# Decoder block on one core: the first token tile of x loaded as two partition halves, issued from SP and from ACT

## The chip, the cores and the metric

The kernel runs on one core of one Trainium2 chip. A core has five engines with an instruction queue each: PE (TensorE, matrix multiplication, with its weight loads shown apart as PEld), DVE (VectorE), ACT (ScalarE), POOL (GpSimd) and SP (SyncE, which here only issues DMA transfers). They run side by side and meet at semaphores; each takes its own instructions strictly in order. DMA transfers between device memory (DRAM) and the core's on-chip memory (SBUF) are issued by an engine's queue and carried out by 16 DMA engines.

The metric is the device time of one execution in microseconds, the median of several runs.

## What is computed

A decoder block on x of shape (8, 112, 512): self-attention, cross-attention to a context, and a gated feed-forward layer, each on a layer norm of x and added to x. Cut to its skeleton, the reference is:

```python
x = x + attn(_layernorm(x), Wq, bq, Wk, bk, Wv, bv, Wo, bo)   # 16 heads, rope, causal, softmax
x = x + xattn(_layernorm(x), ctx, Wq, Wkv_expand, Wout)       # keys and values from ctx, causal
x = x + ffn(_layernorm(x), w_gating, w_linear)                # fp8: gelu(x@w0) * (x@w1) @ w_linear

def _layernorm(x, axis=-1, eps=1e-05):
    m = jnp.mean(x, axis=axis, keepdims=True)
    v = jnp.var(x, axis=axis, keepdims=True)
    return (x - m) / jnp.sqrt(v + eps)
```

Only the very first step, the layer norm of the first 128 tokens, is touched here.

## The kernel before

The 8 x 112 = 896 tokens are treated as 7 tiles of 128 tokens, one token per partition, 512 float32 values (2 KB) each. All of x stays in SBUF as `x_sb` (line 243). Lines 256 and 257 load it, one transfer of 128 partitions and 256 KB per tile, through `load` (line 251), which issues on `nc.sync`, SP's queue. Every other load and every copy inside SBUF that goes by DMA is issued by SP as well; ACT issues none. Three large feed-forward weights are issued by POOL later on.

All work is first written down as a numbered list of operations (`op`, line 57). The text `ORDER` (line 102) then gives the order in which they are emitted, and so each engine's queue. The beginning reads `1 23-24 37 26 40 25 43 85-87 94 22 88 0 89 95-98 90 2-19 91 ...`. Number 1 is a fill of a zero tile by DVE. Numbers 23 to 29 are the loads of x tiles 0 to 6, numbers 37, 40 and 43 the first three quarters of Wv, so SP issues: x tile 0, x tile 1, Wv 0, x tile 3, Wv 1, x tile 2, Wv 2, then Wv 3, the mask, x tiles 6 and 5, Wq 0, and so on. Numbers 2 to 19 are 18 matrix multiplications on the zero tile (line 239, `warm`), which stand at the head of PE's queue.

The path of the first tile, by line:

- line 252, SP: the load; in the trace of the program before, its issue is the first of SP.
- line 300, DVE: `bn_stats` on the tile, then 301 and 302 (mean, variance plus epsilon).
- line 303, POOL: the power -1/2; line 306, DVE: the bias.
- line 307, ACT: the normalised tile `xna`. The load of ACT's function table is placed ahead of it, and the wait for the x tile stands on that table load.
- line 345, PE: four 128 x 128 transposes by `ident`; then the same for tile 1, whose `xna` ACT makes right after the cast of Wv 0 (line 277).
- lines 320 and 321, ACT and DVE: the transposed tile is split into a rounded part `fmh` and a rest `fml`.
- line 359, PE: three matrix multiplications for each product (high by high, low by high, high by low), first for the values with Wv, then the queries and keys with Wq and Wk.

Each weight quarter lands in a staging tile `wst` (line 276), ACT makes the rounded part (277), POOL or DVE the rest (279).

Two mechanisms tie transfers together. Staging tiles come from a set of four (`"ws": 4` in line 98), so a later weight's load waits until an earlier one has been split. And the built program gives every transfer one of eight completion semaphores in turn, whatever queue issues it; an issue first waits until the transfer eight places before it has landed. In the program before, SP's ninth issue (the mask) is the first with such a wait: it waits for x tile 0, the tenth for x tile 1, the twelfth (Wq 0) for x tile 3.

Of the kernel before, what the change touches and what calls it, by code (L numbers as in the profile page):

```python
# [50 lines left out]
class Plan:  # L51
# [5 lines left out]
    def op(self, eng, fn, r=(), w=()):  # L57
        o = Op()
        o.eng, o.fn, o.dma, o.bufs = eng, fn, eng == "sp", []
        for b in dict.fromkeys(k[0] if isinstance(k, tuple) else k for k in (*r, *w)):  # L60
            if isinstance(b, Buf) and b.tags:
                o.bufs.append(b)
                b.left += 1
        self.ops.append(o)
        return o
# [121 lines left out]
def kernel(  # L187
# [5 lines left out]
    nc = tc.nc  # L193
# [9 lines left out]
    op = plan.op  # L203
# [21 lines left out]
    def fixed(t):  # L225
        b = Buf((), None)
        b.ap = t
        return b
# [14 lines left out]
    x_sb = fixed(act.tile([128, NT, D], F32, name="x_sb"))  # L243
# [7 lines left out]
    def load(dst, src, w, r=()):  # L251
        op("sp", lambda: nc.sync.dma_start(out=dst(), in_=src), r=r, w=w)  # L252

    xt = x.rearrange("b s d -> (b s) d").rearrange("(n p) d -> p n d", p=128)
    ot = out.rearrange("b s d -> (b s) d").rearrange("(n p) d -> p n d", p=128)
    for i in range(NT):
        load(lambda i=i: x_sb()[:, i, :], xt[:, i, :], [(x_sb, i)])

    def constant(name, src, shape):
        t = fixed(const.tile(shape, F32, name=name))  # L260
# [396 lines left out]
```

## Time and profile before

| what | value |
|---|---|
| median of 3 runs | 280.43 us (280.15 to 281.84) |
| the profiled execution | 280.48 us, of which the span from first to last instruction is 278.7 us |
| granted TensorE clock | 1.000 |
| PE busy | 273.8 us (98% of the span) |
| DVE, ACT, POOL busy | 214.6, 198.0, 114.4 us |
| transfers | 21.66 MB, 18740 packets, mean 78 GB/s |
| x transfers | 7, each 256 KB, 2.7 us (the first) to 5.8 us from issue to landing |

How to read it: times in the trace count from the first instruction. In the timeline a line gives start, length, engine, line of the kernel, operation, destination and sources, how many were merged, and in brackets the idle time before with what ended it ("the releaser"). "SPq" is SP's queue of transfers; its lengths are those of the issuing, not of the transfer. Time from issue to landing is given in the list of transfers. The chain of waits is followed back from the last instruction; a piece on it has what preceded it as its cause.

### The profile page before, as it was taken

To read this page: it belongs to the slowest core of one execution; us is meant where nothing else is said; L and a number is where in the kernel's file an instruction comes from. 1 tells how busy PE (TensorE), PEld (TensorE's weight loads), DVE (VectorE), ACT (ScalarE), POOL (GpSimd) and SP (SyncE) were. 2 spreads that over 40 slices of the span, in tenths; PEclk is the share of its full clock that TensorE was granted. 3 is DMA by queue.
4 is the path that set the end of the run, shared out by engine and by line. 5 is a ranking of instruction groups with operands and counts; after the bars stand their busy time and mean duration, and the time that the engine had idled before them with its cause. 6 is when DMAs were issued, how large, how long until landed. Compare 5 with 4: busy or idle time off the path is not lost.

```text
span 278.7 us, 7204 instructions
## 1 busy us (share of the span) xinstructions
PE 273.8 (98%) x2472; PEld 213.7 (77%) x2472; DVE 214.6 (77%) x910; ACT 198.0 (71%) x713; POOL 114.4 (41%) x126
## 2 busy tenths in 40 slices
PE   8999999999999999999999999999999999999995
PEld 3688988888887888789888877788888786555454
DVE  3673887899997989996587899989958786573843
ACT  3754141777999999970799999998997756574601
POOL 2787428427784476826532553625410110000100
PEclk9999999999999999999999999999999999999999
DMA  7955753032240413297499500020010100000005
GB/s 220 345 198 167 227 188 111 35 111 83 85 135 3 129 40 115 19 103 66 35 110 108 56 2 2 2 40 5 0 39 2 40 19 2 0 1 2 38 38 188
DMA packets 18740, 21.66 MB, mean 78 GB/s; under 512 B 7056, under 2 KB 11536, under 8 KB 18704
## 3 DMA queue, kind: packets, MB, share of 16 engines
q1 hardware_dynamic: 15584, 18.07, 20.9%
q0 software_dynamic: 3120, 3.15, 12.5%
q8 instruction: 19, 0.31, 0.5%
q14 instruction: 17, 0.14, 0.2%
HBM read 22.39 MB, written 1.84 MB: 87 GB/s over the span
## 4 chain that ended last, share of the span: by engine, by line
PE 88%; DMA 7%; ACT 2%; SPq 1%; issue 0%; POOL 0%; DVE 0%; ACTq 0%; POOLq 0%
PE psm L359 40%; PE psfg L568 18%; PE pspt L439 9%; PE psfo L593 9%; PE pss L416 6%; PE psav L449 5%; DMA wst<-in_Wk_dram 3%; DMA wst<-in_Wq_dram 2%; PE psm L345 2%; DMA x_sb<-in_x_dram 2%; ACT P L428 1%; SPq L252 1%; POOL wqwl L279 0%; ACT xna L307 0%; ACT fmh L320 0%
## 5 line engine op out<-in xcount | busy, mean ns | idle before, releaser
L428 ACT ACTIVATE P<-P,at 112x112 f32<-112x112 f32 x256 | 96.6, 383 | 10.7 <-DVE at L425 10.5
L432 POOL TENSOR_TENSOR P<-P,at 112x448 f32<-112x448 f32 x51 | 48.1, 947 | 53.8 <-DVE at L431 42.7
L425 DVE CUSTOM_DVE_ANT_0 P<-pss,mask 112x112 f32<-112x112 f32 x256 | 56.0, 266 | 2.6 <-PE pss L416 2.3
L428 ACT ACTIVATION_READ_ACCUMULATOR P<-P,at 112x1 f32 x256 | 49.4, 193 | 0.0
L439 PE MATMUL pspt<-ident,P 112*112 112x112 f32 x256 | 36.1, 263 | 0.0
L439 PEld LDWEIGHTS pspt<-ident,P 112*112 112x112 f32 x256 | 26.9, 133 | 9.5 <-issue 2.7
L316 ACT CAST gf<-psfg 128x384 bf16<-128x384 f32 (+1 forms) x45 | 22.9, 530 | 13.7 <-PE psfg L568 13.6
L568 PE MATMUL psfg<-x,wgwl 128*128 128x256 fp8e4 (+1 forms) x192 | 28.7, 291 | 0.0
L568 PE MATMUL psfg<-x,wgwh 128*128 128x256 fp8e4 (+1 forms) x192 | 28.0, 291 | 0.0
L568 PEld LDWEIGHTS <-wgwh 128*128 128x128 fp8e4 x192 | 18.4, 98 | 7.2 <-issue 1.0
L568 PEld LDWEIGHTS <-wgwl 128*128 128x128 fp8e4 x192 | 18.4, 98 | 7.0 <-issue 0.8
L578 DVE TENSOR_TENSOR gf<-gf 128x512 bf16<-128x512 bf16 (+1 forms) x32 | 12.6, 402 | 12.9 <-ACT gf L576 6.9
L316 ACT COPY pts<-pspt 112x448 f32<-112x448 f32 x36 | 18.9, 526 | 4.5 <-PE pspt L439 4.3
L425 DVE DVE_READ_ACCUMULATOR2_ANT at<- 112x1 f32 x256 | 21.3, 83 | 0.0
L576 ACT ACTIVATE gf<-gf 128x512 bf16<-128x512 bf16 (+1 forms) x32 | 17.6, 579 | 5.1 <-DVE gf L316 5.0
L316 DVE COPY pts<-pspt 112x448 f32<-112x448 f32 x28 | 17.3, 618 | 2.7 <-PE pspt L439 2.2
L416 PE MATMUL pss<-k,q 32*112 32x112 f32 x512 | 16.9, 268 | 0.0
L416 PEld LDWEIGHTS pss<-k,q 32*112 32x112 f32 x512 | 14.0, 172 | 3.1 <-issue 2.3
L599 POOL TENSOR_TENSOR x_sb<-x_sb,ob 128x512 f32<-128x512 f32 x1 | 1.2, 1230 | 35.9 <-ACT ob L316 35.9
L593 PE MATMUL psfo<-wlin,a 128*128 128x512 fp8e4 x64 | 15.8, 379 | 0.0
L449 PE MATMUL psav<-pts,v_sb 112*32 112x112 f32 x512 | 15.6, 262 | 0.0
L431 DVE RECIPROCAL at<-at 112x4 f32<-112x4 f32 x64 | 10.8, 172 | 4.9 <-ACT P L428 4.2
(139 smaller groups left out, 612.0 us busy)
## 6 DMA issues: line engine op xcount, KB each, us to landing
qt<-qs SPq DMA_DIRECT2D x32, 112.0 KB, 2.0
x_sb<-in_x_dram SPq DMA_DIRECT2D x7, 256.0 KB, 4.4
out_dram<-x_sb SPq DMA_DIRECT2D x6, 256.0 KB, 2.1
wst<-in_Wv_dram SPq DMA_DIRECT2D x4, 256.0 KB, 5.4
wst<-in_Wq_dram SPq DMA_DIRECT2D x4, 256.0 KB, 5.4
wst<-in_Wk_dram SPq DMA_DIRECT2D x4, 256.0 KB, 4.7
wst<-in_Wo_dram SPq DMA_DIRECT2D x4, 256.0 KB, 3.6
wst<-in_WoutT_dram SPq DMA_DIRECT2D x4, 256.0 KB, 3.2
```

The lines of the kernel that those rows point to most:

```text
L316: lambda e: A.copy(dst(), src()) if e == "act" else V.tensor_copy(dst(), src()), r=r, w=w)
L359: T.matmul(out=out(), lhsT=l(a), rhs=r(b), start=q == 0, stop=q == 3 * tot - 1)
L416: T.matmul(out=banks[r]()[:S, j * S : (j + 1) * S], lhsT=qk[0]()[rs, c, t0 : t0 + S], rhs=qk[1]()[rs, c, t0 : t0 + S], start=True, stop=True)
L425: op("dve", lambda ps=ps, r=r, j=j, Pv=Pv, sm=sm: V.tensor_tensor_reduce(Pv()[:, r, :], ps()[:S, j * S : (j + 1) * S], mask(), -SCALE, BIG ...
L428: op("act", lambda r=r, Pv=Pv, sm=sm: A.activation(Pv()[:, r, :], Pv()[:, r, :], AF.Exp, bias=sm()[:S, r : r + 1], scale=-1.0, accum_out=s ...
L432: op(("pool", "dve"), lambda e, sm=sm, Pv=Pv: LO[e].tensor_tensor(Pv(), Pv(), sm()[:S, 8:12].unsqueeze(2).broadcast_to([S, 4, S]), ALU.mul ...
L439: T.transpose(pt()[:S, r * S : (r + 1) * S], Pv()[:, r, :], ident()[:S, :S])
L449: T.matmul(out=av()[r * 32 : (r + 1) * 32, c * S : (c + 1) * S], lhsT=v_sb()[:, b, h * 32 : (h + 1) * 32], rhs=pts()[:S, r * S : (r + 1) * ...
L568: T.matmul(out=ps()[:, j * n : (j + 1) * n], lhsT=wg()[i][:, c, (m + j) * 128 : (m + j + 1) * 128], rhs=x8()[:, c, t0:t1], start=(c == 0), ...
L576: op("act", lambda gb=gb: A.activation(gb()[:, :w], gb()[:, :w], AF.Gelu_apprx_tanh), w=[(gf, 0)])
L578: op("dve", lambda gb=gb, fb=fb: V.tensor_tensor(fb()[:, :w], gb()[:, :w], fb()[:, :w], ALU.mult), r=[(gf, 0)], w=[(gf, 1)])
L593: T.matmul(out=ps()[:, :wd], lhsT=a8()[:, m, s], rhs=wl()[0][:, m, hs], start=(m == 0), stop=(m == NH - 1))
```

## The change

The loads of tiles 1 to 6 stay as they are. The load of tile 0, at the same place in the order, becomes two transfers of 64 partitions and 128 KB each: partitions 0 to 63 issued on SP's queue, partitions 64 to 127 on ACT's queue, where the issue is now ACT's first instruction.

```diff
+    def first_tile():
+
+        for queue, h in ((nc.sync, slice(0, 64)), (nc.scalar, slice(64, 128))):
+            queue.dma_start(out=x_sb()[h, 0, :], in_=xt[h, 0, :])
+
     for i in range(NT):
-        load(lambda i=i: x_sb()[:, i, :], xt[:, i, :], [(x_sb, i)])
+        if i:
+            load(lambda i=i: x_sb()[:, i, :], xt[:, i, :], [(x_sb, i)])
+        else:
+            op("sp", first_tile, w=[(x_sb, 0)])
```

In the built program nothing else moves: PE, DVE and POOL have the same instructions in the same order, ACT has one more (430 against 429), SP as many transfers as before. The waits change in these places: ACT's table load waits for both halves; SP's eighth issue (Wv 3), which had no wait, waits for the first half; the ninth (the mask) for the second half. From the tenth on each issue waits for the same transfer as before. Lines behind the change are 8 higher.

## The prediction

> **What bounds the kernel now.** I read the page's busy shares first: PE is busy for 273.8 of 278.7 us, so it has 4.9 us of idle time in all, and whatever the change brings has to come out of PE's waits near the start. Next I read the chain of waits, in order of time, for the first 45 us:
>
> ```profile
> 0.74 0.41 SPq L252
> ...
> 2.14 4.44 DMA x_sb<-in_x_dram
> ...
> 6.60 5.55 DMA wst<-in_Wq_dram
> ...
> 12.54 5.75 DMA wst<-in_Wk_dram
> ...
> 19.62 3.98 DMA wst<-in_Wk_dram
> ...
> 24.15 0.82 ACT xna L307
> ...
> 25.02 0.66 PE psm L345 x4
> ```
>
> The chain starts at SP's issues and runs through transfers to 23.60 us, where PE takes over. The x transfer on it is not tile 0. It is the one issued at 2.14 us, the fourth of SP's queue, which is tile 3; its landing lets SP issue Wq 0, and so on. Tile 0 is on the chain only by the 0.41 us that SP spends on issuing it. Then the timeline of the first 16 us, for the path of tile 0 itself:
>
> ```profile
> 0.74 0.88 SPq L252 DMA_DIRECT2D x_sb<-in_x_dram  x2
> 1.19 6.54 PE L239 MATMUL pswarm<-zero 128*128 128x512 bf16 x18 [1.19 <-DVE zero L236]
> 3.45 0.69 DVE L300 BATCH_NORM_STATS2 lna<-x_sb 128x6 f32<-128x512 f32 x1 [2.31 <-DMA x_sb<-in_x_dram]
> 3.50 1.28 ACT L307 ACT_TABLE_LOAD   x1 [3.50 <-DMA x_sb<-in_x_dram]
> ...
> 5.54 0.81 ACT L307 ACTIVATE xna<-x_sb,lna 128x512 f32<-128x512 f32 x1 [0.76 <-DVE lna L306]
> ...
> 6.26 0.60 ACT L277 CAST wvwh<-wst 128x512 fp32r<-128x512 f32 x1
> ...
> 6.77 0.81 ACT L307 ACTIVATE xna<-x_sb,lna 128x512 f32<-128x512 f32 x1
> ...
> 7.36 1.01 PEld L345 LDWEIGHTS psm<-ident,xna 128*128 128x128 f32 x8
> 7.57 1.04 PE L345 MATMUL psm<-ident,xna 128*128 128x128 f32 x8
> ```
>
> The reader is to see two things. Tile 0 has landed by 3.45 us, and its normalised form is ready at 5.54 + 0.81 = 6.35 us. But PE does not take it before 7.36 us, because 18 warm-up matmuls, started by DVE's zero fill and not by x, stand ahead of it in PE's queue until then. So the tile waits for PE for 1.01 us, and PE does not wait for the tile. Last, the busy time by stretches of 1 us, for the DMA share (last but one column) and GB/s (last):
>
> ```profile
> 1.00:2.00 1.00, 0.81 (x2) 0.28 (x3) 0.13 (x1) 0.00 (x0) 0.00 (x0) 1.00 0.22 53
> 2.00:3.00 1.00, 1.00 (x4) 0.43 (x3) 0.00 (x0) 0.00 (x0) 0.00 (x0) 1.00 0.95 277
> 3.00:4.00 1.00, 1.00 (x4) 0.33 (x3) 0.55 (x1) 0.50 (x1) 0.00 (x0) 1.00 1.01 260
> ```
>
> From 2 us on the 16 DMA engines are full (shares of 0.95 and 1.01, and about 1.0 up to 16 us). The bytes of the start are the same before and after, so the train of transfers can only move if its beginning moves.
>
> **The change part by part.** *SP's first issue becomes one of 64 partitions.* Would it be shorter? SP's issues last 0.33 to 0.43 us in the first 13 us. The 0.33 us occurs for 2 KB (bk_t) and for 256 KB (the x tile at 8.44 us) alike, and the mask of 112 partitions took 0.43. So the size of the transfer does not set it. Ends: 0.08 us less (0.41 to 0.33), 0.02 more (0.43); I take 0, since the neighbours at 1.21 and 1.66 us show 0.42 and 0.43. SP's later issues then keep their places, and the chain above its start.
>
> *ACT issues the other half as its first instruction.* No row shows an issue on ACT. Bounds by SP's issues: 0.33 to 0.63 us (the copy to v_sb at 17.77 us). Queued behind it are the table load and everything ACT does; but ACT is idle until 3.50 us, so an issue that starts by about 0.9 us (DVE's first instruction is at 0.86) ends before 1.6 us. It costs 0. If that cover were gone, the 0.76 us in which ACT waits for DVE's L306 after its table load (4.78 to 5.54) would be next.
>
> *The landing of tile 0,* now the later of two halves. Early end: the nearest transfers of half the size, the 112 KB copies qt<-qs, land 2.0 us after issue, where tile 0 took 2.7; that is 0.7 us less, so 2.74 us in place of 3.44. Late end: ACT's half takes as long as Wv 0, the fourth in line at the start, 4.2 us from issue to landing; so 4.94 us, 1.5 us later. I take 2.7 us, no difference: the row is tile 0 itself, which has the DMA engines to itself until tile 1 is issued at 1.21 us, and two halves bring the same 256 KB to the same 16 engines.
>
> What is each worth? Early: DVE's L300, ACT's table load and `xna` of tile 0 move up by as much, and PE still comes at 7.36 us. Tile 1, the second four transposes, gains nothing either, since PE does the two tiles one after the other. Worth 0 for any gain in the landing. Late by L: the table load, `xna` 0, the cast of Wv 0 and `xna` 1 are one queue on ACT, almost without gaps from 5.54 to 7.58 us, so all move by L. The first four transposes stand 1.01 us off. The second four start about half-way through the weight loads' 1.01 us, at 7.36 + 0.5 = 7.86, and `xna` 1 is ready at 7.58: a slack of about 0.3 us. So the price on PE is L - 0.3 us: nothing up to L = 0.3, and 1.2 us at L = 1.5. From 9.45 to 25 us PE runs almost without gaps, so I let nothing of it be won back. Sum for the landing: 0, bounds 0 and +1.2 us.
>
> *Trainium skill, against the row.* The row of the 112 KB copies says that half the size lands 0.7 us sooner. The Trainium skill, page "DMA: Bandwidth & Descriptors", section "Rules for kernel authors", speaks against this very change: of two transfers to disjoint halves of the partitions it says "Don't bother", since both halves are spread over all 16 DMA engines, from two issuing engines as interleaved rings, and it advises one transfer of 128 partitions. By the rule tile 0 would land as before, at 3.44 us, and by the row at 2.74; the sum is the same by both, since PE does not wait for tile 0.
>
> *New waits.* SP's eighth issue, Wv 3, now waits for SP's half, and the ninth, the mask, for ACT's half. Before, SP came to Wv 3 at 4.03 us and to the mask at 4.51. With the halves landed at 3.44 the waits are over 0.59 and 1.07 us before SP comes. At the late end, 4.94, SP would stand still for 0.91 us, with everything queued behind: mask, x tiles 6 and 5, Wq 0. Still the DMA engines would not run dry: the transfer issued last before, Wv 2 at 3.56 us, landed 5.6 us later, at 9.2. Nothing behind is paced by SP's hand alone either, as Wq 0 waits for tile 3, which lands at 6.58. Cost 0; bounds 0 and 0.1 us (Wv 3 landed at about 9.9, and ACT casts it from about 10.3 us on: 0.4 us of slack against a shift that the full engines mostly swallow). DVE's L300 and the table load wait for two semaphores in place of one; what that takes no row shows, and it falls inside the 0.3 us of slack.
>
> *Sum:* SP's issue 0, ACT's issue 0, the landing 0, the waits 0. Against the profiled execution of 280.48 us (span 278.7 and 1.78 around it) that makes 280.5; the median of the three runs is 280.43, so I say 280.4.
>
> **The rivals.** *First: ACT's half lands late (slower).* One mechanism: the first transfer of a queue that the kernel had not used starts late, or its issue is slow, and tile 0 is complete only with it. For it: no row shows an issue on ACT. Against it: ACT has nothing else to do at 0.7 us, and SP's first issue, also the first of its queue, landed soonest of all x transfers. It decides from 0.3 us of lateness on. At 1.5 us late it gives 280.4 + 1.2 + 0.1 = 281.7. To exceed 1% (2.8 us) the half would have to land 3.1 us late, about 6.5 us after the start; that is 5.8 us from issue to landing, which only x tiles behind a full queue took.
>
> *Second: the train of transfers starts earlier (faster).* If SP's first issue takes less, or if two queues get tile 0 out of the way sooner, tile 1, tile 3 and then Wq and Wk on the chain move up. For it: the chain to 25 us is made of these. Against it: the DMA engines are full, and from 9.45 to 25 us PE has only waits of tenths of a microsecond to give up. The price goes from 0.08 us (SP's issue) to 0.7 at most (the whole early end of the landing), so 280.3 to 279.7.
>
> *Third: the change doesn't do what it says.* Both halves are in flight together but share the engines, so tile 0 lands as before; then the time is as forecast, 280.4. It differs from the forecast only in what the profile will show at 3.45 us.
>
> **How the numbers follow.** The forecast, including the third rival, in which nothing that PE waits for moves: 0.74, from 280.0 to 280.9 (the runs shown scatter from 0.28 us below to 1.41 above their median; I take the bulk of that). ACT's half late: 0.15, up to 281.7. The train earlier: 0.08, down to 279.7. What I have not thought of: 0.03. The range that holds 8 in 10 takes in both bounds: 279.7 to 281.7. A change of 1%, 2.8 us, is about the least that a measurement of this kernel tells from none. Within the bounds neither gain nor loss reaches it. Slower by over 1% gets 0.04: of the late case 0.03, for a landing over 3.1 us late, and 0.01 of the unknown. Faster by over 1% gets the other 0.02 of the unknown. Same: 0.94.
>
> **What would show it.** In the changed kernel's profile: DVE's L300 (then L308) on tile 0 starts within 2.7 to 3.7 us; SP's first issues start 0.74, 1.21, 1.66 us as before; ACT's issue ends before 1.6 us; the transposes of L345 (then L353) start at about 7.4 us again, behind 18 warm-up matmuls; and the first 45 us of the chain show the transfers of tile 3, Wq and Wk at the same times. I would be wrong if PE has an idle stretch between the warm-up and the transposes, that is, if ACT's half lands later than 3.7 us; if SP's eighth issue stands waiting for the first half; or if the time changes by more than 1 us while all of the start looks the same, as that would mean a cause outside the start that I have not seen.

## The result, and the profile after

| | median | range | runs |
|---|---|---|---|
| before | 280.47 us | 279.78 to 281.84 | 20 |
| changed | 281.50 us | 280.54 to 283.98 | 20 |

The ratio is 1.0039, with a 95% interval of 1.0021 to 1.0057: the changed kernel is slower by 1.1 us (0.0039 x 280.47). That is far below 1%, but clear of zero; the forecast had been no change. The profiled execution took 282.76 us (span 281.0), 1.3 us more than the median, so its losses are larger than typical. The ratios below leave out two executions that were over 1.5% slower than the fastest of their kernel, one of e6 (456.93 us) and one of the kernel before on the chip of e1 to e4 (283.81 us).

The timeline of the changed kernel's first 4 us, SP's and ACT's queues, and what waits for tile 0:

```profile
0.73 0.57 ACTq L259 DMA_DIRECT2D x_sb<-in_x_dram  x1
...
0.73 0.60 SPq L259 DMA_DIRECT2D x_sb<-in_x_dram  x1
...
1.40 0.80 SPq L252 DMA_DIRECT2D x_sb<-in_x_dram  x1
...
2.24 0.51 SPq L252 DMA_DIRECT2D wst<-in_Wv_dram  x1
...
2.79 0.43 SPq L252 DMA_DIRECT2D x_sb<-in_x_dram  x1
...
3.93 1.28 ACT L315 ACT_TABLE_LOAD   x1 [3.93 <-DMA x_sb<-in_x_dram]
3.94 0.69 DVE L308 BATCH_NORM_STATS2 lna<-x_sb 128x6 f32<-128x512 f32 x1 [2.80 <-DMA x_sb<-in_x_dram]
```

The same issues of Wv 0 and tile 3 in the timeline of the kernel before:

```profile
1.66 0.43 SPq L252 DMA_DIRECT2D wst<-in_Wv_dram  x1
2.14 0.43 SPq L252 DMA_DIRECT2D x_sb<-in_x_dram  x1
```

SP's issue of half a tile took 0.60 us, where the whole tile had taken 0.41, and the next two took 0.80 and 0.51 in place of 0.42 and 0.43. So tile 3 was issued at 2.79 us (before: 2.14). Tile 0 was complete at 3.94 us, 0.49 later than before; in the list of transfers ACT's half landed 2.6 us after issue (3.3 us on the clock), SP's 3.1 us after (3.8). In the chain of waits the 0.65 us stay:

```profile
0.73 0.60 SPq L259
...
1.40 0.80 SPq L252
...
2.24 0.51 SPq L252
...
2.79 4.33 DMA x_sb<-in_x_dram
...
7.14 5.74 DMA wst<-in_Wq_dram
...
13.27 5.79 DMA wst<-in_Wk_dram
...
22.51 4.71 DMA cos<-in_cosT_dram
```

Wq lands at 12.88 (before: 12.15), Wk at 19.06 (18.29). Then something new stands on the chain: cos, issued when it was before (22.51 against 22.45 us), lands 4.7 us after its issue, where it took 2.9. DVE (whose rope operations, the rotation of queries and keys, need cos), POOL, ACT and PE follow (timeline from 27 to 42 us):

```profile
27.31 0.68 DVE L398 SCALAR_TENSOR_TENSOR q<-psm,bq_t,cos 128x448 f32<-128x448 f32 x1 [3.63 <-DMA cos<-in_cosT_dram]
...
39.37 1.14 POOL L406 TENSOR_TENSOR k<-k,qt 128x448 f32<-128x448 f32 x1 [2.31 <-DMA qt<-qs]
...
40.55 0.81 ACT L315 ACTIVATE xna<-x_sb,lna 128x512 f32<-128x512 f32 x1 [2.27 <-POOL k L406]
...
41.41 0.65 PE L353 MATMUL psm<-ident,xna 128*128 128x128 f32 x4 [1.18 <-ACT xna L315]
```

The same steps in the kernel before:

```profile
25.42 0.68 DVE L390 SCALAR_TENSOR_TENSOR q<-psm,bq_t,cos 128x448 f32<-128x448 f32 x1 [2.49 <-DMA cos<-in_cosT_dram]
...
37.90 0.82 ACT L307 ACTIVATE xna<-x_sb,lna 128x512 f32<-128x512 f32 x1
...
39.80 0.60 PE L345 MATMUL psm<-ident,xna 128*128 128x128 f32 x4
```

DVE's first rope operation starts at 27.31 us (before: 25.42), and PE stands idle for 1.18 us before tile 4's transposes, which it had started at 39.80 without waiting. From 16 us on this is PE's only wait of over half a microsecond; a smaller one, 0.3 us for DVE's `k`, lies inside the first block of scores (48.86 us).

Milestones of PE, read from the timelines (us), for this kernel and those of the experiments below. Each row is one profiled execution:

| profile | Wv 0 issued | tile 6's transposes | tile 4's | second block of scores | span | span less scores |
|---|---|---|---|---|---|---|
| before | 1.66 | 25.02 | 39.80 | 56.39 | 278.7 | 222.3 |
| changed | 2.24 | 25.35 | 41.41 | 58.47 | 281.0 | 222.5 |
| changed, again (e17) | 2.24 | 24.89 | 41.53 | 58.40 | 280.8 | 222.4 |
| halves by columns (e18) | 1.67 | 25.09 | 39.81 | 56.40 | 278.9 | 222.5 |
| halves by columns (e5) | 1.65 | 24.88 | 40.57 | 57.42 | 280.0 | 222.6 |
| both halves on SP (e2) | 2.63 | 25.07 | 40.29 | 58.42 | 280.9 | 222.5 |
| SP later (e6) | 2.13 | 25.27 | 40.03 | 57.52 | 280.1 | 222.6 |
| tile 1 on ACT too (e13) | 1.40 | 24.76 | 39.73 | 56.37 | 278.8 | 222.4 |
| changed, cos early (e7) | 2.24 | 25.99 | 40.78 | 57.37 | 279.8 | 222.4 |
| both halves on ACT (e10) | 1.19 | 27.69 | 42.45 | 59.04 | 281.5 | 222.5 |
| SP later, 64 rows (e14) | 2.45 | 26.42 | 41.19 | 57.71 | 280.2 | 222.5 |
| three tiles, rows (e15) | 3.29 | 26.40 | 41.18 | 58.07 | 280.7 | 222.6 |
| three tiles, columns (e16) | 2.60 | 26.00 | 40.72 | 57.34 | 279.9 | 222.6 |

The last column is the point: what comes after the second block of scores takes 222.3 to 222.6 us in every row. All that these executions differ by arises in the first 59 us.

### The profile page after: what moved, and what is told of

The parts are those of the page before. It is cut to its first block, busy times and chain, and to the rows that moved or that the text cites. A ratio compares the mean times of both kernels' runs of the same rounds, so it can differ in the third digit from the quotient of the medians.

```text
span 281.0 us, 7206 instructions
## 1 busy us (share of the span) xinstructions
PE 274.7 (98%) x2472; PEld 213.8 (76%) x2472; DVE 214.1 (76%) x910; ACT 198.3 (71%) x713; POOL 114.5 (41%) x126
## 4 chain that ended last, share of the span: by engine, by line
PE 79%; DMA 11%; SPq 3%; DVE 2%; ACT 2%; issue 1%; POOL 0%; DVEq 0%; ACTq 0%; POOLq 0%
PE psm L367 33%; PE psfg L576 17%; PE pspt L447 9%; PE psfo L601 9%; PE pss L424 6%; PE psav L457 5%; DMA qt<-qs 4%; DMA wst<-in_Wk_dram 2%; DMA wst<-in_Wq_dram 2%; DMA cos<-in_cosT_dram 2%; DMA x_sb<-in_x_dram 2%; SPq L252 1%; SPq L404 1%; PE psm L353 1%; ACT P L436 1%
```

## The experiments

The first theory, T, was that two queues issuing side by side slow each other. It fell at once, and its successors, P (64 partitions make an issue slow) and T2 (what costs is the lateness of SP's train of transfers), had rivals of their own: S and H (the division as such costs), C (chance in the warm-up), L and W (tile 0's landing, the start), V (only cos). Ratios are to the kernel before on the same chip, with 95% intervals.

### Which part slows the issue: e1 to e4

e1 is the changed kernel once more. The edits of the others, in `first_tile`:

```diff
 # e2_both_sp
-for queue, h in ((nc.sync, slice(0, 64)), (nc.scalar, slice(64, 128))):
+for queue, h in ((nc.sync, slice(0, 64)), (nc.sync, slice(64, 128))):
 # e3_whole_act
+for queue, h in ((nc.scalar, slice(0, 128)),):
 # e4_act_small
+nc.sync.dma_start(out=x_sb()[:, 0, :], in_=xt[:, 0, :])
+nc.scalar.dma_start(out=spare[64:128, 0:4], in_=xt[64:128, 0, 0:4])
```

> The changed kernel itself a second time, to see which of its differences come back. Theory T (two queues issuing side by side make SP's issues slower): SP's first three issues again take about 0.60, 0.80 and 0.51 us in place of 0.41, 0.42 and 0.43, Wv 0 is issued at about 2.2 us (before: 1.66), tile 0 lands near 3.9 us (before: 3.45), and the time is 0.5 to 1.5 us above the kernel before. Theory C (the loss of the profile is chance, above all the 15 instead of 13 half-speed warm-up matmuls, which set PE back by 0.34 us): the issues are back near 0.43 us or the warm-up is back at 13, and the time is within 0.3 us of the kernel before.

> The two halves stay, but SP issues both; ACT issues nothing. Theory T: no issue is slowed, each takes 0.41 to 0.43 us; SP's train is later by one issue, so x tile 1 is issued at about 1.66 and Wv 0 at about 2.1 us (0.47 later than before), tile 0 lands at 3.4 to 3.9 us. If it is the lateness of the train that costs, the time is 0.3 to 1 us above the kernel before. Theory S (the split costs by itself, by two transfers of 64 partitions, one more semaphore and the new wait of Wv 3): as slow as the changed kernel, plus about 1 us, with issues of 64 partitions that are themselves longer than 0.43 us.

> Tile 0 in one transfer of 128 partitions, issued by ACT; SP's first issue is x tile 1. Theory T: ACT's and SP's first issues run side by side at 0.73 us and are both slowed to about 0.6 us, the next of SP to about 0.8; as SP has one issue less, Wv 0 is issued at about 2.2 - 0.6 = 1.6 us, about as before, and the time is within 0.4 us of the kernel before. Theory S: no split, so issues of 0.41 to 0.43 us on both queues, the train of transfers 0.47 us earlier (Wv 0 issued at 1.2 us), and the time equal or up to 0.5 us lower.

> Tile 0 in one transfer by SP, as before; ACT issues beside it a load of 64 partitions of 16 bytes each into a spare tile that nothing reads (added work). Theory T: the issue on ACT alone slows SP's first issues by 0.2 to 0.4 us each, Wv 0 at about 2.2 us, and the time is 0.5 to 1.2 us above the kernel before. Theory S (or that the bytes of the half matter): SP's issues stay at 0.41 to 0.43 us, Wv 0 at 1.66, and the time is within 0.3 us of the kernel before.

e1: 1.0018 (0.9985 to 1.0051), by itself unclear; but SP's issues came back (0.60 and 0.80 to the hundredth, then 0.48), with a warm-up of 6.34 us, shorter than the 6.54 of the kernel before, so C does not explain them. e2: 1.0011 (0.9989 to 1.0034), so no loss is shown there, though S expected one, and T too if lateness costs; its median, 281.09 us, is 0.09 below that of the kernel before on its chip. e3: 0.9964 (0.9942 to 0.9987). e4: 1.0000 (0.9974 to 1.0026). The timeline of SP's queue in e2:

```profile
0.74 1.23 SPq L259 DMA_DIRECT2D x_sb<-in_x_dram  x2
2.01 0.59 SPq L252 DMA_DIRECT2D x_sb<-in_x_dram  x1
2.63 0.43 SPq L252 DMA_DIRECT2D wst<-in_Wv_dram  x1
```

Two halves on SP alone, with ACT silent, take 0.60 and 0.57 us, and the whole tile behind them 0.59. In e4, on the other hand, ACT's issue of 64 partitions takes 0.54 us and SP's whole tiles beside it 0.39 and 0.41; in e3 both queues issue whole tiles side by side at 0.39 and 0.41 us. So T is wrong: in these runs it is the transfer of 64 partitions that is slow to issue, on either queue, not two queues at once.

### The form of the transfer: e5, e11, e17, e18

```diff
 # e5_columns, e18_columns
+for queue, h in ((nc.sync, slice(0, 256)), (nc.scalar, slice(256, 512))):
+    queue.dma_start(out=x_sb()[:, 0, h], in_=xt[:, 0, h])
 # e11_sizes (added work)
+nc.sync.dma_start(out=x_sb()[:, 0, :], in_=xt[:, 0, :])
+for k, n in enumerate((128, 112, 96, 64, 32, 16)):
+    nc.scalar.dma_start(out=spare[0:n, k * 16 : k * 16 + 16], in_=xt[0:n, 0, 0:16])
```

> Two transfers of 128 KB from SP and ACT as in the change, with the same waits, but halved by columns: 128 partitions x 256 values each. Theory P (what is slow is the issue of a transfer of 64 partitions, 0.57 to 0.60 us on either queue against 0.39 to 0.43 for 128, and it makes SP's train late): both issues take 0.39 to 0.43 us, Wv 0 is issued at 1.66 us as before, and the time is within 0.4 us of the kernel before. Theory H (half-size transfers or a split over two queues cost by themselves): issues of about 0.6 us again, Wv 0 at about 2.2 us, and a time 0.5 to 1 us above before.

> One look for the cost of an issue. The kernel before, with six small loads added on ACT at its start, of 128, 112, 96, 64, 32 and 16 partitions of 64 bytes each, into a spare tile that nothing reads (added work; its total time says nothing). Theory P (issues of fewer partitions than 128 are slower): 0.39 to 0.43 us for 128 and above 0.5 us for 64; open for the others. Rival: all take about the same, and the slow issue is only the first of a queue or one beside another's.

> The changed kernel on the same chip as the halves by columns next to it, so that the two can be set side by side. Theory P: 0.5 to 1.3 us above the kernel before, SP's first issues at 0.6, 0.8 and 0.5 us once more.

> Tile 0 halved by columns over SP and ACT (as in e5). Theory P: within 0.4 us of the kernel before and 0.4 us or more below the changed kernel of the same chip. Theory H (two transfers over two queues cost as such): equal to the changed kernel within 0.3 us.

e11: ACT's issues took, for 128, 112, 96, 64, 32 and 16 partitions of 64 bytes each, 0.41, 0.46, 0.45, 0.53, 0.59 and 0.32 us. P holds for 64 against 128. These six stand behind one another, and behind a slow issue the next one is slow too (0.80 and 0.59 us above), so for the smaller ones the row mixes the size with what went before; e4's 0.54 us is 64 partitions with nothing ahead. e5: 1.0009 (0.9987 to 1.0031); its median is 0.53 us above the kernel before, a little more than the 0.4 that P allowed. Side by side on one chip, e17, the changed kernel: 1.0037 (1.0008 to 1.0065); e18, the halves by columns: 0.9997 (0.9973 to 1.0020). SP's queue in e17, then in e18:

```profile
0.73 0.61 SPq L259 DMA_DIRECT2D x_sb<-in_x_dram  x1
1.40 0.79 SPq L252 DMA_DIRECT2D x_sb<-in_x_dram  x1
2.24 0.53 SPq L252 DMA_DIRECT2D wst<-in_Wv_dram  x1
```

```profile
0.74 0.40 SPq L259 DMA_DIRECT2D x_sb<-in_x_dram  x1
1.20 0.42 SPq L252 DMA_DIRECT2D x_sb<-in_x_dram  x1
1.67 0.43 SPq L252 DMA_DIRECT2D wst<-in_Wv_dram  x1
```

The same two transfers of 128 KB, on the same two queues, with the same waits, keep SP's train in its place when they have 128 partitions, and no loss is left in the ratio; the medians of e17 and e18 are 0.7 us apart (281.64 and 280.92), though the two intervals overlap a little. Tile 0 still landed no earlier than in one piece (3.75 us against 3.45). The division brings nothing either way; its form costs. One profile speaks against too simple a reading: e5 has SP's train in its place and still waits for tile 4,

```profile
40.57 0.66 PE L353 MATMUL psm<-ident,xna 128*128 128x128 f32 x4 [0.81 <-ACT xna L315]
```

after cos had landed 4.0 us after its issue. So that wait also occurs without a late train.

### Does a late train alone cost: e6, e14, and e15 against e16

```diff
 # e6_sp_later (added work)
+nc.sync.dma_start(out=x_sb()[:, 0, :], in_=xt[:, 0, :])
+nc.sync.dma_start(out=spare[:, 0:4], in_=xt[:, 0, 0:4])
 # e14_sp_64 (added work): in place of the last line
+nc.sync.dma_start(out=spare[64:128, 0:4], in_=xt[64:128, 0, 0:4])
 # e15_three_rows: tiles 0, 1 and 3, all on SP
+for h in (slice(0, 64), slice(64, 128)):
+    nc.sync.dma_start(out=x_sb()[h, i, :], in_=xt[h, i, :])
 # e16_three_columns: the same by columns
+for h in (slice(0, 256), slice(256, 512)):
+    nc.sync.dma_start(out=x_sb()[:, i, h], in_=xt[:, i, h])
```

> The kernel before, with one small added load on SP behind x tile 0 (128 partitions of 16 bytes into a spare tile that nothing reads): tile 0 as early as before, the rest of SP's train later by one issue, about 0.45 us. Theory V (a late train makes cos land late; DVE's rope on Wq waits for cos; the exchange qt, POOL and ACT's xna of tile 4 follow; PE waits for that tile's transposes near 41 us): cos lands at 26 to 27.3 us in place of 25.4, PE waits 0.3 to 1.3 us between 40 and 60 us, the time is 0.3 to 1 us above before. Theory W (the loss is at the start, from tile 0's later landing and the later start of PE): no wait of PE beyond 0.2 us between 40 and 60 us, and a time within 0.3 us of before.

> The kernel before, with one small added load on SP behind the whole tile 0, of 64 partitions of 16 bytes into a spare tile that nothing reads: as e6, but with 64 partitions in place of 128. Theory P: this issue takes 0.5 to 0.6 us (128 partitions: 0.41) and the next of SP is longer too, so Wv 0 is issued at 2.3 to 2.7 us (e6: 2.13, before: 1.66), as late as in the change or later. Theory T2: with the train 0.6 to 1 us late and nothing split, the time is 0.6 to 1.6 us above before. Theory L: no split, so within 0.4 us of before.

> The form of the transfer alone, enlarged: the kernel before with tiles 0, 1 and 3 each as two halves of 64 partitions, all issued by SP. Theory P (64 partitions make the issue slow): six issues of about 0.6 us each, so that Wv 1, issued at 2.61 us before, is issued at about 0.74 + 6 x 0.62 + 0.5 = 5 us; the time is 1.5 to 3.5 us above before, and 0.7 us or more above the same with halves by columns.

> The same three tiles as two halves by columns (128 partitions x 256 values), all issued by SP: as many transfers, bytes and waits as with halves by partitions. Theory P: six issues of about 0.41 to 0.43 us, Wv 1 issued at about 4.0 us, the time 0.7 to 2.5 us above before and 0.7 us or more below the halves by partitions. Theory H (half-size transfers cost as such, whatever their form): issues and time as with the halves by partitions, within 0.4 us.

e6: 1.0029 (1.0001 to 1.0057), with tile 0 whole, at its place, and ACT silent. e14: 1.0035 (1.0012 to 1.0058); the added issue took 0.59 us and the next 0.57, Wv 0 came at 2.45. So in these two a late train without any split costs as much as the change did. e2 doesn't fit: its train was later still (Wv 0 at 2.63), and its time was not clearly longer. e6's profile pays at a place of its own, the first block of scores:

```profile
48.63 0.66 PE L426 MATMUL pss<-k,q 32*112 32x112 f32 x16 [0.64 <-DVE k L408]
```

Over all profiles the two do go together. In the eight with Wv 0 issued at 2.13 us or later and cos at its old place, DVE's first rope operation starts at 27.00 to 27.76 us; in five of the seven others that load cos there (e11 with its six added loads left aside) it starts at 24.62 to 25.61. The exceptions are e5 (26.78) and e10 (28.80), whose tile 0 was itself late. e15: 1.0065 (1.0041 to 1.0089); e16: 1.0037 (1.0015 to 1.0059). SP's queue in e15, then in e16:

```profile
0.73 2.51 SPq L258 DMA_DIRECT2D x_sb<-in_x_dram  x4
3.29 0.59 SPq L252 DMA_DIRECT2D wst<-in_Wv_dram  x1
3.92 1.11 SPq L258 DMA_DIRECT2D x_sb<-in_x_dram  x2
5.07 0.58 SPq L252 DMA_DIRECT2D wst<-in_Wv_dram  x1
```

```profile
0.74 1.82 SPq L258 DMA_DIRECT2D x_sb<-in_x_dram  x4
2.60 0.43 SPq L252 DMA_DIRECT2D wst<-in_Wv_dram  x1
3.08 0.91 SPq L258 DMA_DIRECT2D x_sb<-in_x_dram  x2
4.03 0.43 SPq L252 DMA_DIRECT2D wst<-in_Wv_dram  x1
```

With as many transfers, bytes and waits, four issues take 2.51 us by rows and 1.82 by columns; Wv 1 is issued 1.04 us later, and the medians differ by 0.7 us (282.54 and 281.83). The two intervals overlap a little, so of the timings alone the direction is likely rather than certain.

### Where the lateness is paid: e7, e8, e12, e10, e13, e9

e7, e8 and e12 move the load of cos in the order (`ORDER`) up behind sin: in the changed kernel, in the kernel before, and in e6.

```diff
 # e7, e8, e12, e9
-... 285 30 33 63p ... 71 73 32 79 ...
+... 285 30 33 32 63p ... 71 73 79 ...
 # e10_both_act
+for queue, h in ((nc.scalar, slice(0, 64)), (nc.scalar, slice(64, 128))):
 # e13_tile1_act: the change, and besides
+nc.scalar.dma_start(out=x_sb()[:, 1, :], in_=xt[:, 1, :])
 # e9_act_cos: e3 with the move of cos
```

> The changed kernel, with the load of cos moved up in SP's order, from behind the first quarter of Wo to right behind sin. Theory V: cos lands 2 to 4 us earlier, DVE's first rope operation starts when PE has the product (23 to 24 us, in place of 27.3), the wait of PE for tile 4's transposes near 41 us (1.18 us) is gone, and the time is 0.8 to 1.5 us below the changed kernel, thus at 280.0 to 280.7, though Wv 0 is still issued at 2.2 us. Theory W: the start is unchanged, so the time stays at about 281.5.

> The kernel before with the same move of cos. Theory V: DVE's first rope operation starts at about 22.5 to 23.5 us in place of 25.4; as PE waited little there in the profile, the time is equal or up to 1 us lower, and the runs above 281.5 us become rare; e7 and e8 then differ by no more than 0.4 us. Theory W: the same time as before, and e7 stays about 1 us above e8.

> The kernel before with the small added load on SP behind x tile 0 (as in e6: the train later by 0.47 us, no split, ACT issues nothing) and with cos moved up behind sin (as in e7). Theory T2, with two routes from a late train to PE (tile 1 at the start, and cos with tile 4 near 41 us): the second route is closed, the first stays, so PE's transposes of tile 1 start near 8 us and the time is 0.2 to 0.9 us above the kernel before with cos early (280.41), thus 280.6 to 281.3, below e6 without the move. Theory V alone (only cos matters): as fast as cos early without the delay, 280.4 within 0.3 us.

> Both halves of tile 0 are issued by ACT, one after the other; SP's first issue is x tile 1. Theory T2 (what counts is when SP's train of whole transfers runs; tile 0's own landing hardly counts): ACT's two issues take 0.5 to 0.6 us each, tile 0 lands at 4 to 4.9 us (later than in the change, 3.9), yet SP's issues take 0.41 to 0.43 us from 0.74 us on, Wv 0 at 1.2 us, there is no wait of PE beyond 0.3 us between 40 and 60 us, and the time is 280.2 to 280.8, 0.5 to 1 us below the changed kernel. Theory L (tile 0's later landing, or the split as such, costs): slower than the changed kernel, by up to 1 us, as tile 0 lands later still.

> The changed kernel, with the load of tile 1 issued by ACT too, behind ACT's half of tile 0. SP then has one issue less, which makes up for its slow first ones. Theory T2: SP's first issue takes 0.6 us and the next 0.8, so Wv 0 is issued at 1.4 and tile 3 at about 2.2 us (before: 2.14; in the change: 2.79); with the train back in its place the time is within 0.5 us of the kernel before, if tile 0 and tile 1 land by about 3.9 and 5 us. Theory L: the split and two queues still cost, 0.8 to 1.5 us above before; the two tiles on ACT's queue land late, as the halves did there when both were issued by ACT (7.1 us).

> Tile 0 whole on ACT's queue (as in e3, SP's train 0.47 us earlier) and cos moved up behind sin. Theory T2: both routes from the train to PE have slack, the time is 280.0 to 280.5, 0.2 to 0.9 us below the kernel before, with little scatter (no run above 281.5 us). Theory L: tile 0 lands at 4.1 us as in e3, so no gain: equal to before within 0.3 us.

e7: 1.0033 (1.0006 to 1.0060), though DVE's first rope operation starts at 23.99 us and PE's wait near 41 us is gone. V alone is wrong. In that profile the loss sits at the start (PE's timeline):

```profile
8.31 0.63 PE L353 MATMUL psm<-ident,xna 128*128 128x128 f32 x4 [1.76 <-POOL lna L311]
9.45 0.66 PE L353 MATMUL psm<-ident,xna 128*128 128x128 f32 x4 [0.51 <-ACT xna L315]
```

The warm-up was short there (5.36 us), tile 0 was complete at 4.04 us, tile 1 only at 6.51, and PE had nothing to do for 1.76 us. Tile 0 was held up by tile 1, whose statistics stand ahead of tile 0's bias in DVE's queue:

```profile
6.51 0.69 DVE L308 BATCH_NORM_STATS2 lna<-x_sb 128x6 f32<-128x512 f32 x1 [1.37 <-DMA x_sb<-in_x_dram]
...
7.12 0.20 DVE L314 TENSOR_SCALAR lna<-lna 128x1 f32<-128x1 f32 x1
```

Tile 1 was issued at 1.40 us as in the other profiles of the change, but landed 5.1 us later, where it took 3.3 to 3.6 in those. So this loss comes from a slow landing, not from a later issue; why it was slow isn't shown. e8: 0.9984 (0.9960 to 1.0008). e12: 1.0008 (0.9989 to 1.0028), between e8 and e6; its profile shows PE waiting 1.6 us for tile 6 at 26.58 us, behind Wk on ACT. That profile is e12's slowest execution (282.33 us; median 281.06). So there are four places where PE met a late input in these profiles: tiles 0 and 1 at 7 to 9 us, tile 6 at 25 us, tile 4 at 41 us, and the first block of scores at 48 us. The milestones above show e10, e14, e15 and e16 paying mostly by tile 6, the changed kernel at tile 4, and e2 and e6 for the greater part behind tile 4.

e10: 1.0077 (1.0044 to 1.0109), the slowest of all. ACT's two issues took 1.19 us, and behind SP's train the second half landed at 7.08 us:

```profile
10.13 0.63 PE L353 MATMUL psm<-ident,xna 128*128 128x128 f32 x4 [2.73 <-POOL lna L311]
11.26 0.66 PE L353 MATMUL psm<-ident,xna 128*128 128x128 f32 x4 [0.51 <-ACT xna L315]
```

T2 had expected a gain and missed: tile 0's landing does cost once its lateness exceeds PE's slack. e13: 1.0024 (1.0002 to 1.0047). Its profile, with the train back in place, agrees with the kernel before at every milestone (56.37 against 56.39 us, 280.56 us in all), as T2 wants; its median, 281.49 us, does not. So with the train in place a loss of 0.0024 is left, just clear of zero; what the other executions of e13 lost isn't shown. e9: 0.9994 (0.9976 to 1.0013), so no gain; with e3's 0.9964 on another chip, a version that beats the kernel before is not established.

## Why the prediction was right or wrong

The forecast of no change was wrong, by 1.1 us in 280; the time lies in the range and within 1%. That the range held it is luck: its upper end was priced for ACT's half landing late, which did not happen.

- **SP's first issue: wrong, and the step that failed.** The prediction bounded it by 0.33 to 0.43 us, on rows of 112 and 128 partitions alone, and concluded that "the size of the transfer does not set it". It measured 0.60 and 0.61 us in three profiles, and the issues behind it grew as well, so the train was 0.65 us late: SP's first three issues started at 0.73, 1.40 and 2.24 us, not at 0.74, 1.21 and 1.66. A row that gave a hint was in the trace of before, SP's issues of qt<-qs, which have 64 partitions (0.53 and 0.59 us for the first two):

```profile
26.76 1.17 SPq L396 DMA_DIRECT2D qt<-qs  x2
```

  I had used that very row for its landing time and not for its issue, and the 0.63 us of the copy to v_sb for ACT's bound and not for SP's. It was no more than a hint, as these are copies inside SBUF: that copy to v_sb has 96 partitions, and a load of 96 took 0.45 us in e11.
- **The second rival: right place, wrong sign.** It said that the train sets the first 25 us, and priced only the case in which the train comes earlier. Turned round, its shift of up to 0.7 us holds the 0.65 us by which the train moved, but not the price: it counted the same 0.7 us as the most that the time could change, and the medians differ by 1.0 us.
- **The first rival: wrong.** ACT's half was the earlier to land (3.3 us against 3.8); the prediction's sign of being wrong, a half landing after 3.7 us, came true by SP's half. (Wv 0, from which the late end was taken, is the third of SP's issues, not the fourth; tile 3, the fourth, took 4.4 us.) ACT's issue (0.57 us, in the bounds) was hidden, as said.
- **The slack on PE: right.** In e10 tile 0 was 3.63 us late (7.08 less 3.45). The prediction's slack of 1.01 us for tile 0 gives 2.62 us; PE's transposes started 2.56 us later (10.13 against 7.57). For the change itself, 0.49 us late, it gives 0.2 us, and e17 shows tile 1's transposes at 8.21 us, where the kernel before had them at about 8.09 (7.57 and half of 1.04). In the first profile of the change PE waited for neither tile, as its warm-up was 0.35 us longer: the slack moves with the warm-up.
- **The new waits of SP: right.** In the first profile of the change Wv 2 and Wv 3 were issued back to back (0.91 us for both at 4.22); nothing waited for a half.
- **"From 9.45 to 25 us PE runs almost without gaps": true, and not enough.** I looked for covers up to 25 us and not at tile 4 near 40 us, whose margin in the profile before was 1.1 us (`xna` ready at 38.72, used at 39.80). Nor is 1% the least that tells a change from none, as the prediction had it: with 20 executions each the interval is about 0.2% to either side.
- **The advice not to split.** The Trainium skill, "DMA: Bandwidth & Descriptors", section "Rules for kernel authors", advises one transfer of 128 partitions, because two halves share the DMA engines. The runs agree in the outcome: tile 0 came at 3.94 us, not 2.74. That the halves would take longer to issue is not part of that rule; it is what cost here.

Shown: the slow issue (all profiles with a 64-partition half of tile 0 on SP), that a late train by itself can cost as much (e6, e14), and that of the two forms the halves by rows cost and those by columns don't in the ratio (e17, e18, e5). Against lateness as the whole account stand e2 (late, no loss shown) and e13 (in place, a loss left). Not tested is whether halves by rows also make a later transfer land slowly, apart from the lateness: cos did so in the profiles of the change and of e2, but not in e10, e13 and e15, which have such halves too. Open: why an issue of 64 partitions takes longer than one of 128, why the one after it does too, and how the loss comes about in a typical execution, as all three profiled ones of the change took 282.6 to 282.8 us, a microsecond above its median.

## What to carry to other kernels

Before halving a load, look for rows with the same number of partitions wherever in the trace they stand, and price the issue by them, or measure it by a small added load as in e4. If two queues are wanted, halve the columns and keep the 128 partitions. A queue that issues everything in order hands its delay on (here 0.65 us at tile 3 became 0.7 to 0.8 at the landings of Wq and Wk), so look for the next consumer with little margin over the whole stretch that the queue feeds, and price both signs.

## What the runs showed of the hardware

- The time of an issue rose from 0.41 us at 128 partitions to 0.53 at 64 and 0.59 at 32, and fell to 0.32 at 16 (e11, 64 bytes per partition, one behind the other); halves by columns, with 128 partitions, took 0.39 to 0.41 (e5, e18).
- In all three profiles of the changed kernel and in e2, cos landed 4.7 to 5.6 us after its issue, against 2.7 to 4.0 in the other kernels that load it at the old place. In these four the last bytes came slowly. By stretches of half a microsecond, the last two columns being the share of the 16 DMA engines and GB/s, e17 first, then e18:

```profile
26.00:26.50 0.50, 0.50 (x4) 0.47 (x3) 0.00 (x0) 0.00 (x0) 0.00 (x0) 1.00 0.07 25
26.50:27.00 0.50, 0.50 (x5) 0.41 (x3) 0.00 (x0) 0.36 (x1) 0.00 (x0) 1.00 0.07 23
27.00:27.50 0.50, 0.50 (x3) 0.19 (x2) 0.00 (x0) 0.50 (x2) 0.16 (x1) 1.00 0.07 25
```

```profile
25.00:25.50 0.50, 0.50 (x7) 0.44 (x5) 0.00 (x0) 0.29 (x1) 0.50 (x2) 1.00 0.49 184
25.50:26.00 0.50, 0.50 (x5) 0.47 (x4) 0.47 (x1) 0.27 (x1) 0.50 (x2) 1.00 0.03 12
```

  A share of 0.07 is about one engine of sixteen (0.0625), at 25 GB/s, so one engine seems to finish about 1.5 us after the rest; this is inferred from the share, as the engines aren't shown one by one. cos landed at the end of that stretch (21.93 and 5.6 us). Why the engine lags is open.
- The 18 warm-up matmuls took between 5.36 us (e7) and 7.01 us (e9) from profile to profile, while the granted clock shows 1.00 throughout: they run at a pitch of 0.43 us at first and faster later, and where that turns differs from profile to profile. So the earliest moment at which PE can take tile 0 differs by up to 1.6 us, whatever the loads do.
